# A convolution with three outputs from four products of 171 columns, and work moved into the attention's last unit

## The chip, the cores and the metric

The kernel runs on one core of a Trainium2 chip. The metric is the device time of one execution in microseconds, as the median of several. The core has five engines that run side by side and wait for each other through semaphores: TensorE (PE, matmuls; PEld is its weight load), VectorE (DVE), ScalarE (ACT), GpSimd (POOL) and SyncE (SP), which here issues nearly all DMA transfers. Each engine, SP too, works through its own instructions in order.

## The reference

Inputs are x (4 batches, 1024 tokens, 512 features), a context tensor (4, 2048, 512), a side column (4, 1024, 1) and weights. Three blocks follow each other, and each adds its input and is normalised over the 512 features:

```python
x = _layernorm(x + attn(x))     # 32 heads of 16; q, k and v are two chained linear layers each
x = _layernorm(x + xattn(x, ctx_1024, fside))
x = _layernorm(x + ffn(x))      # quantised activations, ternary weight
```

The middle block treats the 1024 tokens as 512 hidden channels and 512 cell channels, and the 512 features as positions:

```python
xp = concatenate([hid, z1h], axis=2)              # one more position in front
out = uss + conv_general_dilated(xp, weight) + bias   # 512 -> 2048 channels, kernel size 2
it, ot, gt, ft = split(out, 4, axis=1)
ct = sigmoid(ft) * z0c + sigmoid(it) * tanh(gt)
ht = sigmoid(ot) * tanh(ct)
```

So the convolution is, for every output position s, w0 x[s] + w1 x[s+1] over a padded row of 513 positions, where w0 and w1 are 512x2048 matrices.

## The kernel before

**Attention.** `attention` runs 32 units, one for each batch and group of four heads, with a step u = -1 ahead of them. A unit's inner loop has 32 half steps h (line 638). In each, TensorE makes scores twice: once with queries on partitions (`nat`, line 421, for the row maxima of the next unit, reduced on VectorE in line 437) and once with keys on partitions (`scores`, line 491), from which ScalarE makes exponentials (line 502); every fourth h, `weigh` (line 517) multiplies these by the values. Fill pieces go between: projections of queries and keys (line 346), of values (line 371), and in the last units output projections of batches 0 and 2 (`out_piece`, line 400, which calls `Handed.project`, line 180). The last unit, u = 31, has no `nat` work left: it runs the branch of line 610, 16 steps i with two score groups each and a weighing at every even i, and no fill.

**What goes round a unit.** The four stages of `normalise` (line 536) move a unit's denominators out and back through DRAM, multiply on GpSimd (line 564) and store the result to `attn_d` with eight DMAs (line 574). Packed projections lie in tiles of the pool `packs`; DMAs spread them into the query and key tiles (line 332).

**The hand-over.** `Handed` holds what is prepared for the tail during the attention: the convolution's first weight tile (`load_conv(0)`, at i = 1 of the last unit), its tap sums on GpSimd (`sum_taps`, line 147), the small constants and the ternary weight (`load_rest`, line 149). `outs` (line 587) lists the output projections that the attention does: all eight tiles of batch 0 and five of batch 2. After the last weighing, lines 675 to 681 put out, in this order, the first stage of the last unit's `normalise`, the first norm of batch 0 (`first_norm`, line 119: statistics, a square root on ScalarE, eight normalisations on VectorE), and the other stages.

**The tail.** A list of due times (`after(steps, work)` and `step()`) puts side work between the steps of TensorE's work. Lines 902 to 911 begin it: two context loads, output projection of tile 5 of batch 2, the convolution's operands of batch 0 (`fir_parts`), tiles 6 and 7, the load of batch 1's attention, the first norm of batch 2. Then, for the batches (0, 2) and after that for (1, 3): four rounds t; a round is four gates g for each of the two batches, so eight gates of 128 output channels by 512 positions. In each round the next weight tile is loaded at its first gate and its taps are summed two gates later (line 936). After the fourth gate of a batch, `combine` (line 777) makes the cell and hidden channels with six GpSimd operations and a tanh on ScalarE, and then loads the context tile that comes two later (`load_ctx(k + 2)`), for the context tiles have two buffers. After four rounds, `feed_forward` runs for the 16 tiles of both batches; between the two pairs come the output projections of batches 1 and 3.

**A gate.** The convolution gets two outputs from three products of 256 columns. With pairs of neighbouring positions (x0, x1) and the next x2, `fir_parts` makes x0 - x1, x1 and x2 - x1 on VectorE and ScalarE, and `sum_taps` makes w0 + w1. The first output is w0 (x0 - x1) + (w0 + w1) x1, the second w1 (x2 - x1) + (w0 + w1) x1. So a gate (line 756) is three products over four blocks of 128 channels, 12 matmuls of 256 columns. VectorE adds the first two products to the context tile (line 767) and the third, common to both, to both halves (line 768), and ScalarE applies the gate's function (line 769). The two accumulator tags `ps_c` and `ps_a` have two buffers each.

Of the kernel before, what the change touches and what calls it, by code (L numbers as in the profile page):

```python
# [14 lines left out]
P = 128  # L15
# [5 lines left out]
VW = HD + 1  # L21
EPS = 1e-5
# [29 lines left out]
class Handed:  # L52
# [3 lines left out]
    def __init__(self, tc, a, shared, attn_d, eps):  # L56
        self.eps = eps
        self.nc, self.a, self.shared, self.attn_d = tc.nc, a, shared, attn_d
        self.big, self.y, self.stats = {}, {}, {}
# [59 lines left out]
    def first_norm(self, b):  # L119
# [3 lines left out]

        def part(t0):
            if t0 == 0:
                made.extend(self.norm_stats(self.stats[b], self.shared, f"1_{b}"))
# [4 lines left out]
        return x1, [lambda t0=t0: part(t0) for t0 in range(0, NT, 2)]  # L131

    def load_conv(self, m, pool):


        if m % 2 == 0:
            w = self.shared.tile([P, 6, S], F32, tag="qk3", name=f"w{m}")
        else:
            w = pool.tile([P, 6, S], F32, tag="w", name=f"w{m}")
        w = w.rearrange("p a s -> p (a s)").rearrange("p (i k o) -> p i k o", i=FT, k=3)  # L140
# [4 lines left out]
    def sum_taps(self, w):  # L145
        for i in range(FT):
            self.nc.gpsimd.tensor_add(w[:, i, 2, :], w[:, i, 0, :], w[:, i, 1, :])

    def load_rest(self):
# [7 lines left out]
        nc.gpsimd.dma_start(self.w_f, a["ternary_wT"].rearrange("(t p) f -> p t f", p=P))  # L157
# [7 lines left out]
    def prepare_rest(self):  # L165
        nc = self.nc
        nc.gpsimd.tensor_scalar_add(self.w_f, self.w_f, -1.0)
# [28 lines left out]
def attention(ctx, tc, a, attn_d, ident, shared, hand):  # L196
# [35 lines left out]
    for n, pool in ((3, shared), (1, once)):  # L232
        t = pool.tile([P, 2 * n, S], F32, tag=f"qk{n}", name=f"qk{n}")
        for i in range(n):
# [3 lines left out]
            k_ts.append(t[:, n + i, :])  # L238

# [10 lines left out]
    packs = ctx.enter_context(tc.tile_pool(name="packs", bufs=1))  # L250
# [19 lines left out]
    for which, (w, v, dst) in enumerate((("wq", "vq", b_q), ("wk", "vk", b_k), ("wv", "vv", None))):  # L270
# [22 lines left out]
        if which == 2:  # L293
            bias()
            b_d = dpool.tile([D], F32, tag="b_v", bufs=1, name="b_vd")
            nc.gpsimd.dma_start(b_d.rearrange("(t p) -> p t", p=P), dst)
            nc.gpsimd.dma_start(b_v, b_d.partition_broadcast(P))
# [84 lines left out]
    packed_of = {}  # L382

    def qk_pieces(p, which):


        def piece(t0, n):
            if t0 == 0:
                packed_of[p, which] = packs.tile(
                    [P, S], F32, tag=f"packed{which}", name=f"packed{p}_{which}"  # L390
                )
            project(p, which, t0, n, packed_of[p, which])

        parts = [(0, 176), (176, 176), (352, 176), (528, 176), (704, 160), (864, 160)]
        return [lambda part=part: piece(*part) for part in parts]
# [191 lines left out]
    outs = [(0, t) for t in range(NT)] + [(2, t) for t in range(5)]  # L587
# [3 lines left out]
    for piece in qk_pieces(0, 0) + qk_pieces(0, 1) + folds[:5]:  # L591
        piece()

    for u in range(-1, NU):
# [15 lines left out]
        if u == -1 or u + 1 == NU:  # L610
            total, done = len(fill), 0
            for i in range(HS // 2):
# [8 lines left out]
                if u >= 0 and i % 2 == 1:  # L621
                    weighing.append((u, i // 2))
                if i == 1 and u >= 0:
# [364 lines left out]
```

## Time and profile before

| | us |
|---|---|
| median of 3 runs | 2502.4 (2501.43 to 2502.85) |
| the profiled execution | 2499.28 |
| its span, first to last instruction | 2497.5 |

The granted TensorE clock was 0.999 of full speed. Read from the trace by stage, in us from the span's start:

| stage | from | to | PE busy | DVE busy | ACT busy | POOL busy |
|---|---|---|---|---|---|---|
| convolution of batches 0 and 2, most of it | 2040 | 2136 | 96.00 | 35.86 | 22.05 | 40.69 |
| their feed-forward | 2136 | 2202 | 62.51 | 60.98 | 22.33 | 6.72 |
| output projections of 1 and 3 | 2202 | 2257 | 55.00 | 42.92 | 1.80 | 5.39 |
| convolution of batches 1 and 3 | 2257 | 2424 | 167.00 | 65.59 | 36.04 | 62.32 |
| their feed-forward | 2424 | 2497.5 | 62.03 | 65.19 | 22.59 | 6.69 |

An fp32 matmul stands in the trace as two matmul records, each with its weight load. Matmuls are pipelined, so the busy time of one record is longer than the spacing of two; the spacing is read from the chain of work that ended last, whose pieces give a start, a length and how many records it holds. In groups, the numbers after the bar are the busy time in all and the mean in ns of one, and behind the second bar stands the engine's idle time just before them and what ended it.

### The profile page before, as it was taken

The numbers are of one execution on the slowest core, as the hardware profiler recorded it, in microseconds if no ns is written. First come the engines' busy times: TensorE is split into PE (matmuls) and PEld (weight loads), VectorE is DVE, ScalarE is ACT, GpSimd is POOL, SyncE is SP. The second block draws the span as 40 slices with busy tenths as digits, with TensorE's granted clock in tenths as the row PEclk, the third lists the DMA queues.
The fourth block names the chain that finished last, engine by engine and source line by source line (L and its number), as shares of the span: only waits on it lengthen the run. The fifth ranks groups of instructions, "written<-read, shape, count | busy, mean of one in ns | idle before, by whom it ended". The sixth has DMA issues, their size and how long they took to land.

```text
span 2497.5 us, 58830 instructions
## 1 busy us (share of the span) xinstructions
PE 2476.3 (99%) x24956; PEld 1766.8 (71%) x24956; DVE 1670.5 (67%) x2055; ACT 1309.9 (52%) x2560; POOL 293.5 (12%) x230
## 2 busy tenths in 40 slices
PE   9999999999999999999999999999999999999998
PEld 6677777777777777777777776777776688548874
DVE  3767777776777777777777777777775433875348
ACT  1166666666666666666666666666656411401132
POOL 2000000000000000000000002000021245102530
PEclk9999999999999999999999999999999999999999
DMA  7001111111110211111111114011111323230301
GB/s 246 17 11 20 20 25 53 21 24 20 25 24 16 58 21 20 20 22 23 20 23 22 23 22 134 16 25 21 54 45 50 115 85 118 89 147 31 120 19 68
DMA packets 80086, 120.71 MB, mean 48 GB/s; under 512 B 38560, under 2 KB 38560, under 8 KB 79824
## 3 DMA queue, kind: packets, MB, share of 16 engines
q1 hardware_dynamic: 78608, 114.59, 16.2%
q8 instruction: 196, 3.21, 0.5%
q0 software_dynamic: 640, 1.31, 0.2%
q10 hardware_dynamic: 576, 1.05, 0.1%
q14 instruction: 66, 0.54, 0.1%
HBM read 80.77 MB, written 18.35 MB: 40 GB/s over the span
## 4 chain that ended last, share of the span: by engine, by line
PE 94%; DVE 5%; DMA 0%; issue 0%; ACT 0%; SPq 0%; POOL 0%; DVEq 0%; POOLq 0%
PE nat L421 21%; PE av L517 19%; PE st L491 18%; PE proj L346 10%; PE pc L765 9%; PE v L371 5%; PE pa L765 4%; PE po L185 4%; PE fold L307 1%; PE pf L844 1%; DVE y L849 1%; DVE y L875 1%; DVE y L115 1%; DVE stats L850 1%; DVE xq L830 1%; PE fold L361 1%
## 5 line engine op out<-in xcount | busy, mean ns | idle before, releaser
L437 DVE TENSOR_REDUCE mx<-nat 128x2 f32<-128x1024 f32 x1008 | 1187.5, 1219 | 453.8 <-PE st L491 424.2
L502 ACT ACTIVATE at<-st 128x512 f32<-128x512 f32 x2016 | 1042.7, 602 | 609.9 <-PE st L491 605.7
L421 PE MATMUL nat<-qk 32*128 32x512 f32 x4032 | 1012.8, 614 | 1.0 <-DVE mx L437 1.0
L491 PE MATMUL st<-qk 32*128 32x256 f32 x8064 | 998.9, 387 | 0.0
L491 PEld LDWEIGHTS st<-qk 32*128 32x128 f32 x8064 | 656.1, 184 | 46.0 <-issue 3.6
L517 PE MATMUL av<-at,v_sb 128*32 128x256 f32 x8192 | 497.4, 382 | 0.6 <-ACT at L502 0.6
L421 PEld LDWEIGHTS nat<-qk 32*128 32x128 f32 x4032 | 343.3, 184 | 171.4 <-DVE mx L437 117.2
L517 PEld LDWEIGHTS av<-at,v_sb 128*32 128x32 f32 x8192 | 241.4, 109 | 221.6 <-ACT at L502 90.2
L564 POOL TENSOR_TENSOR o_n<-o_sb,rbc 128x512 f32<-128x512 f32 x64 | 94.9, 1506 | 1643.9 <-DMA rbc<-rec_d 1356.6
L346 PE MATMUL proj<-xT,w_qk 128*128 128x176 f32 (+1 forms) x1536 | 270.2, 320 | 0.7 <-ACT w_qk L312 0.7
L346 PEld LDWEIGHTS proj<-xT,w_qk 128*128 128x128 f32 x1536 | 223.7, 189 | 64.6 <-ACT at L502 60.0
L765 PE MATMUL pc<-xf,w 128*128 128x256 f32 x1024 | 231.9, 379 | 2.9 <-DVE u L767 2.9
L765 PEld LDWEIGHTS pc<-xf,w 128*128 128x128 f32 x1024 | 194.3, 190 | 30.4 <-DVE u L767 3.3
L769 ACT ACTIVATE u<-u,b_c 128x512 f32<-128x512 f32 x64 | 46.2, 722 | 207.9 <-DVE u L768 207.9
L767 DVE TENSOR_TENSOR u<-pc,u 128x512 f32<-128x512 f32 x64 | 44.2, 691 | 142.3 <-PE pc L765 134.4
L371 PE MATMUL v<-w_v,xT 128*128 128x256 f32 x512 | 126.0, 391 | 0.0
L765 PE MATMUL pa<-xf,w 128*128 128x256 f32 x512 | 120.9, 379 | 0.0
L844 PE MATMUL pf<-w_f,xq_t 128*128 128x512 f32 x256 | 115.6, 595 | 4.5 <-DVE y L849 3.0
L185 PE MATMUL po<-w_o,big 128*128 128x256 f32 (+1 forms) x360 | 117.5, 477 | 0.0
L371 PEld LDWEIGHTS v<-w_v,xT 128*128 128x128 f32 x512 | 92.5, 189 | 34.4 <-ACT at L502 16.6
L530 DVE TENSOR_TENSOR o_sb<-av,o_sb 128x256 f32<-128x256 f32 x128 | 54.3, 424 | 92.5 <-PE av L517 92.5
L765 PEld LDWEIGHTS pa<-xf,w 128*128 128x128 f32 x512 | 97.3, 190 | 13.2
(94 smaller groups left out, 1111.6 us busy)
## 6 DMA issues: line engine op xcount, KB each, us to landing
qk<-packed SPq DMA_DIRECT2D x256, 64.0 KB
w<-in_conv_wT SPq DMA_DIRECT2D x32, 512.0 KB
u<-in_ctx SPq DMA_DIRECT2D x16, 1024.0 KB
xT<-in_xT SPq DMA_DIRECT2D x16, 512.0 KB
rbc<-rec_d SPq DMA_DIRECT2D x128, 64.0 KB
attn<-o_n SPq DMA_DIRECT2D x256, 32.0 KB
big<-attn SPq DMA_DIRECT2D x4, 2048.0 KB
y<-in_x SPq DMA_DIRECT2D x4, 2048.0 KB
```

The costliest lines, as they stand in the source:

```text
L185: nc.tensor.matmul(pt, attn_t[:, f, t * P : (t + 1) * P], self.w_o[:, f, cols], start=f == 0, stop=f == FT - 1)
L346: nc.tensor.matmul(pt[:, 0:n], w[:, f, gg * P : (gg + 1) * P], xts[b][:, f, cols], start=f == 0, stop=f == FT - 1)
L371: nc.tensor.matmul(pt, xts[b][:, f, t * P : (t + 1) * P], w_v[:, f, cols], start=f == 0, stop=f == FT - 1)
L421: nc.tensor.matmul(pts[n], q_ts[u % 4][r : r + 32, qt * P : (qt + 1) * P], k_ts[u % 4][r : r + 32, kh * 512 : kh * 512 + 512], start=True, ...
L437: nc.vector.tensor_reduce(mxs[u][:, qt, 2 * pair : 2 * pair + 2, kh], pt, AX.X, ALU.max, negate=True)
L491: nc.tensor.matmul(st[:, k * QW : k * QW + QW], k_ts[u % 4][r : r + 32, kt * P : (kt + 1) * P], q_ts[u % 4][r : r + 32, qq * QW : qq * QW ...
L502: nc.scalar.activation(at, st, AF.Exp, scale=0.25)
L517: nc.tensor.matmul(av[32 * j : 32 * j + 32, :], v_sb[b % 2][:, kt, c * VW : c * VW + 32], ats[u, 2 * i + n // 2, j][:, n % 2 * QW : n % 2 ...
L530: nc.vector.tensor_add(o, av, o)
L564: nc.gpsimd.tensor_mul(o_n[:, :, half * 256 : half * 256 + 256], o_sb[:, cols].rearrange("p (s e) -> p e s", e=2), rbc[:, cols].rearrange( ...
L765: nc.tensor.matmul(dst, w[:, i, tap, o : o + P], xf[:, tap, i, :], start=i == 0, stop=i == FT - 1)
L844: nc.tensor.matmul(pt, xq_ts[b, t][:, f, :], hand.w_f[:, f, :], start=f == 0, stop=f == FT - 1)
```

## The change

Three outputs now come from four products of 171 columns (a third of 513, the padded row). For positions x0, x1, x2 of a triple and the next x3 the four products are p0 = w0 (x0 - x2), p1 = w1 (x3 - x1), m = (w0 + w1)(x1 + x2) and n = (w0 - w1)(x2 - x1). The outputs are p0 + m/2 + n/2, m/2 - n/2 and p1 + m/2 + n/2. A gate is 16 matmuls of 171 columns. The context tiles and `load_ctx` go to `Handed` and have 513 columns, with the last set to zero by GpSimd; the weight tiles have four taps; the gate's VectorE work is four operations.

```diff
-        for dst, tap in ((pt[:, 0, :], 0), (pt[:, 1, :], 1), (pa, 2)):
-            if tap == 1 and between:
+        ends = ps_c.tile([P, 2, 256], F32, tag="c", name=f"pc{b}_{t}_{g}")
+        mids = ps_a.tile([P, 2, 256], F32, tag="a", name=f"pa{b}_{t}_{g}")
+        for tap in range(4):
+            if tap == 2 and between:
                 between()
+            pt = (ends, mids)[tap // 2][:, tap % 2, 0:TR]
             for i in range(FT):
-                nc.tensor.matmul(dst, w[:, i, tap, o : o + P], xf[:, tap, i, :], start=i == 0, stop=i == FT - 1)
-        ug = u[:, g, :].rearrange("p (m e) -> p e m", e=2)
-        nc.vector.tensor_add(ug, pt, ug)
-        nc.vector.tensor_add(ug, pa.unsqueeze(1).to_broadcast([P, 2, 256]), ug)
+                nc.tensor.matmul(pt, w[:, i, tap, o : o + P], xf[:, tap, i, :], start=i == 0, stop=i == FT - 1)
+
+        ug = u[:, g, :].rearrange("p (m e) -> p e m", e=3)
+        outer = ug[:, 0:3:2, :]
+        nc.vector.tensor_add(outer, ends[:, :, 0:TR], outer)
+        m, n = (mids[:, i, 0:TR] for i in range(2))
+        both = n.unsqueeze(1).to_broadcast([P, 2, TR])
+        nc.vector.scalar_tensor_tensor(outer, both, 0.5, outer, ALU.mult, ALU.add)
+        nc.vector.scalar_tensor_tensor(ug[:, 1, :], n, -0.5, ug[:, 1, :], ALU.mult, ALU.add)
+        all3 = m.unsqueeze(1).to_broadcast([P, 3, TR])
+        nc.vector.scalar_tensor_tensor(ug, all3, 0.5, ug, ALU.mult, ALU.add)
```

The taps and the operands:

```diff
     def sum_taps(self, w):
-        for i in range(FT):
-            self.nc.gpsimd.tensor_add(w[:, i, 2, :], w[:, i, 0, :], w[:, i, 1, :])
+        for tap, op in ((2, ALU.add), (3, ALU.subtract)):
+            for i in range(FT):
+                self.nc.gpsimd.tensor_tensor(w[:, i, tap, :], w[:, i, 0, :], w[:, i, 1, :], op)
+
+    def fir_parts(self, b, x1, pool):
...
+        xf = pool.tile([P, 4, FT, TR], F32, tag="xf", name=f"xf{b}")
+        x = x1[:, 0:FT, :].rearrange("p t (m e) -> p t e m", e=3)
+        x0, x1, x2 = (x[:, :, e, :] for e in range(3))
+        tt = self.nc.vector.tensor_tensor
+
+        def first():
+            tt(xf[:, 0, :, :], x0, x2, ALU.subtract)
+            tt(xf[:, 2, :, :], x1, x2, ALU.add)
+
+        def second():
+            tt(xf[:, 3, :, :], x2, x1, ALU.subtract)
+            self.nc.vector.memset(xf[:, 1, :, TR - 1 : TR], 0.0)
+            tt(xf[:, 1, :, 0 : TR - 1], x0[:, :, 1:TR], x1[:, :, 0 : TR - 1], ALU.subtract)
```

Work moved into the attention's last units: the output projections of tiles 5 to 7 of batch 2 as six half pieces, the statistics of batch 0's first norm (at h = 5 of unit 30), its normalisation and operands (steps i from 3 on), and the first context load.

```diff
-    outs = [(0, t) for t in range(NT)] + [(2, t) for t in range(5)]
+    outs = [(0, t) for t in range(NT)] + [(2, t) for t in range(NT)]
...
+                if u >= 0 and i % 2 == 0 and out_pieces:
+                    out_pieces.pop(0)()
+                if u >= 0 and i > 2 and firsts:
+                    firsts.pop(0)()
...
+                if i == 3 and u >= 0:
+                    hand.load_ctx(0, None)
...
+                if h == 5 and u == 30:
+                    hand.x1[0], firsts = hand.first_norm(0)
+                    firsts.pop(0)()
+                    hand.xf[0], parts = hand.fir_parts(0, hand.x1[0], shared)
+                    firsts.extend(parts)
...
-    for part in hand.first_norm(0)[1]:
+    hand.x1[2], parts = hand.first_norm(2)
+    for part in parts:
         part()
...
-    x1[0] = hand.big[0].rearrange("p (t s) -> p t s", t=NT)
-    load_ctx(0)
     load_ctx(1)
     big1 = bigs.tile([P, NT * (D + 1)], F32, tag="big", name="big1")
-    project_out(2, (5,))
-    fir_parts(0)
-    project_out(2, (6, 7))
-    hand.load_attention(1, big1)
-    first_norm(2)
+    firs[2], parts = hand.fir_parts(2, x1[2], fir)
+    for m, part in enumerate(parts):
+        after(m + 1, part)
+    after(5, lambda: hand.load_attention(1, big1))
```

The first norm of batch 2 is therefore the one put out after the last weighing. For batches 1 and 3 the operands' two parts come as separate side work, due within five steps (batch 1) or three (batch 3) of the norm's start.

Three more edits concern where things lie and by which queue they come. The packed projections move from their own pool into two more rows of the tile that holds queries and keys of three of four units (`qk3`), and the weight tiles of even number use that tile's place. The value bias goes through DRAM on SP's queue, after the first projections, instead of on GpSimd's. The ternary weight is loaded by SP as integers and turned to fp32 in the GpSimd operation that subtracts one, where a GpSimd DMA converted it before; the scratch for GpSimd's DMAs is set to 2048.

```diff
-        nc.gpsimd.dma_start(self.w_f, a["ternary_wT"].rearrange("(t p) f -> p t f", p=P))
+        nc.sync.dma_start(self.w_f.bitcast(mybir.dt.int32), a["ternary_wT"].rearrange("(t p) f -> p t f", p=P))
...
-        nc.gpsimd.tensor_scalar_add(self.w_f, self.w_f, -1.0)
+        nc.gpsimd.tensor_scalar_add(self.w_f, self.w_f.bitcast(mybir.dt.int32), -1.0)
...
-        t = pool.tile([P, 2 * n, S], F32, tag=f"qk{n}", name=f"qk{n}")
+        t = pool.tile([P, 8 if n == 3 else 2, S], F32, tag=f"qk{n}", name=f"qk{n}")
...
+        if n == 3:
+            packs = t[:, 6:8, :]
...
+    nc.sync.dma_start(b_d.rearrange("(t p) -> p t", p=P), b_vc)
+    nc.sync.dma_start(b_v, b_d.partition_broadcast(P))
```

## The prediction

> **What bounds the kernel now.** I read the page first (busy shares, then the chain that ended last), then the chain in order of time over the convolution and over the start, then the timeline where the attention ends, then busy time by window.
>
> ```profile
> PE 94%; DVE 5%; DMA 0%; issue 0%; ACT 0%; SPq 0%; POOL 0%; DVEq 0%; POOLq 0%
> ...
> L765 PE MATMUL pc<-xf,w 128*128 128x256 f32 x1024 | 231.9, 379 | 2.9 <-DVE u L767 2.9
> ...
> L765 PE MATMUL pa<-xf,w 128*128 128x256 f32 x512 | 120.9, 379 | 0.0
> ```
>
> The chain is TensorE for 94%. In the convolution its only idle time is 2.9 us, once. Every fp32 matmul has two records, so 1,024 + 512 records are 768 matmuls: 64 gates of 12. The busy means (379 ns) overlap; a price has to be read from the chain, which gives the pace:
>
> ```profile
> 33.67 14.16 PE proj L346 x96
> ...
> 2202.14 54.93 PE po L185 x128
> 2257.07 3.45 PE pc L765 x16
> 2260.52 1.73 PE pa L765 x8
> 2262.25 3.45 PE pc L765 x16
> ```
>
> A gate is 3.45 + 1.73 = 5.18 us, 0.216 us a record of 256 columns; 512 columns take 54.93/128 = 0.429. So a column costs (0.4291 - 0.2158)/256 = 0.833 ns and a record 2.5 ns besides. The first row is the nearest to what comes: the 48 projection matmuls of the start, of 176 and 160 columns (on average 170.7), each record with its own 128x128 weight load.
>
> Where the attention ends:
>
> ```profile
> 1955.98 10.57 PE L185 MATMUL po<-w_o,big 128*128 128x512 f32 x24
> ...
> 1973.88 0.94 SPq L754 DMA_DIRECT2D u<-in_ctx  x2
> ...
> 1979.02 0.69 DVE L767 TENSOR_TENSOR u<-pc,u 128x512 f32<-128x512 f32 x1 [7.88 <-DMA u<-in_ctx]
> ...
> 1979.77 3.72 PE L765 MATMUL pc<-xf,w 128*128 128x256 f32 x16 [2.86 <-DVE u L767]
> ```
>
> TensorE does three output projections, starts gate 0 at 1966.4, and after two gates stands still for 2.86 us: both PSUM buffers are full, VectorE waits for the first context tile, and that load stood in SP's queue behind the last unit's attention stores.
>
> **The gates (the large term).** A gate becomes 16 matmuls of 171 columns, 32 records. By the two slopes a record is 2.5 + 171 x 0.833 = 145 ns, so 4.64 us; by the projection row 14.16/96 = 147.5 ns, so 4.72 (that row holds the slow first record). Gain per gate 0.54 or 0.46, times 64: **-34.4** or -29.3 us. I take -34.4, since the row's excess belongs to its first record, and keep both.
>
> [...] 216 ns is the whole spacing today, and projections ran at 147.5 ns a record with a load for each (the page's mean load of line 346, 189 ns, is longer than that spacing, so it overlaps). [...]
>
> VectorE takes the gate out of PSUM with four operations instead of two. From 256 elements at 424 ns (L530) and 512 at 691 (L767): 157 ns + 1.043 an element. So 342, 342, 171 and 513 elements: 0.51 + 0.51 + 0.34 + 0.69 = 2.06 us against 1.38. That lies beside 4.64 us of TensorE, except where nothing follows. After the very last product of a pair of batches three of them (1.54 us) stand ahead of the feed-forward's first quantisation, where one (0.69) stood:
>
> ```profile
> 2136.34 0.70 DVE u L768
> 2137.70 0.81 ACT xq L828
> ```
>
> +0.85 twice, **+1.7 us**. Ends: 0, if VectorE's backlog there is recovered[...].
>
> The scalar_tensor_tensor form and a stride of three elements are not in the trace. A stride of two is: L767 takes 691 ns, as the contiguous L849 does. [...]
>
> **GpSimd.** Eight tap operations per weight tile instead of four (1.27 each): 10.2 us for 5.0. Behind them in its queue stand combine's operations, behind these the next context load:
>
> ```profile
> 2025.93 5.00 POOL L147 TENSOR_TENSOR w<-w 128x512 f32<-128x512 f32 x4 [7.07 <-DMA w<-in_conv_wT]
> ```
>
> Counted from the start of an eight-gate round (about 2011): taps from +15 to +25; combine about 7.5, so the load goes out at +33, lands some 5 us later (the first context loads took that) at +38. VectorE asks for it at 37.1 + 2.3 = +39.4; TensorE stalls only two gates after the round begins, at +46.4. The memset of one column adds 0.1. Cost 0, with 8 us of cover. The first round is tighter: its weight tile is issued behind the attention stores, about 18 us in, taps end near +35, the context goes out near +42 and lands near +47, against +46.4. I take **+1 us**, ends 0 and +4.
>
> **The moved output projection.** Six half pieces go into the last unit. There ScalarE is nearly full, and weighings follow each other every 4.27 us (8.55 for two, in the second view):
>
> ```profile
> 1930.00:1940.00 10.00, 10.00 (x156) 6.93 (x152) 1.11 (x3) 9.54 (x20) 2.64 (x2) 1.00 0.11 30
> ```
>
> (A window: busy PE, weight load, VectorE, ScalarE, GpSimd, clock, DMA share, GB/s.) The chain there:
>
> ```profile
> 1928.44 1.96 PE av L517 x32
> ...
> 1936.99 1.96 PE av L517 x32
> ```
>
> TensorE's own work there is about 3.93 us (av 1.86, two scores' 2.07), so 0.34 is free. A piece in earlier units costs 1.94 with its change of layout; 1.94 - 0.34 = 1.6, six times +9.6. At the boundary 10.4 us (1955.98 to 1966.38) go, and the 2.86 us stall goes, since context 0 is now loaded during the unit: one SP issue of 0.4 us behind the denominator transfers (there until 1928.5), its memset on an idle GpSimd. The doubled taps of the first weight tile run there from 1923.7 to about 1934, ahead of the attention scaling, which waits for its data until 1937.4. Late next is the second context tile: issued some 18 us after the last weighing, landing near +23, with gate 4 asking at 23.2 and a stall only from 27.9. Norm and tap operands of batch 0 (before: 1956.5 to 1965.6) run on a VectorE busy a tenth in that window. Sum 9.6 - 10.4 - 2.9 = **-3.7**, ends -5 (more hidden) and -2.
>
> **The early deviations** cost ScalarE a table load, 0.30 us and a load back (each 1.28 in the trace) amid exponentials in unit 30, and put 0.63 us of bn_aggr ahead of VectorE's reductions. ScalarE has 0.7 to 1.8 us idle in every 3.83; four score buffers cover more. Ends 0 and +2.9, taken **+1**. A gain is excluded: it adds work there, and what it takes away lay under the output projection.
>
> **At no cost.** The value bias goes to SP behind sixteen row transfers (issued until 55.4); its store took 8.4 us and its broadcast 6.4, so it lands near 70; first use 82.0. The next xT, queued behind it, slips from 55.5 to about 64, first read near 166. Ternary weights: one SP issue more in unit 24, where the 5.4 us GpSimd pass had an idle engine. Operands of the other batches: four VectorE operations of 684 elements (0.87) for two of 1.23 and a ScalarE copy, in rounds with slack; their two steps end before the second batch's gates. Attention reload five gates later: first read at 2202. Packed projections now inside the query/key tile: same lifetimes.
>
> **Sum.** -34.4 + 1.7 + 1 - 3.7 + 1 = -34.4 us. The profiled execution took 2499.28 (span 2497.5 and 1.8 around it), so 2464.9; on the median of 2502.4, 3.1 above it, **2468.0**.
>
> **Rivals.**
> 1. GpSimd's chain becomes a wait in every round: contexts 10 us later than reckoned, beyond the 8 us cover, 2 us in six rounds, 2480. For: the taps double while the round shrinks by 4.3 us. Against: the margin. 0.10.
> 2. More is hidden: pieces vanish in ScalarE's waits, deviations and end free: -34.4 - 5 = -39.4, 2463. 0.08.
> 3. Slower: VectorE becomes the bound through 12-byte strides. Its other work in the second convolution is (65.6 - 32 x 1.38)/32 = 0.67 us a gate, so it decides from 3.97 us a gate, 1.9 times my price, and the kernel is slower from about 4.5[...]. For: the stride is unseen. [...] 0.04.
> 4. The change doesn't do what it says: packed rows in one tile with queries and keys bring false waits, 2 us in 32 projections, +64 - 34, 2532. Against: queries and keys of three units share that tile already, and the projections show 0.7 us idle in all. 0.03.
>
> My forecast has 0.73, 0.02 is left for anything else that just cancels. Of no change one can tell 0.2%, 5 us. Faster 0.91, same 0.02, slower 0.07. Range: bounds of the sum, -39.4 and -29.3 + 2.8 + 4 - 2 + 2.9 = -21.6, so 2463 to 2481; a little more below for the profile's offset: 2460 to 2480.
>
> **What would show it.** A gate at 4.64 us in the chain, records 145 ns apart; VectorE's four operations 2.06 us; no TensorE idle before gate 2; last unit near 47 us instead of 37; feed-forward beginning 0.85 later after the last product. Wrong if records stand at 190 ns, if chain rows in the convolution name GpSimd or the context load, or if VectorE's strided operations exceed 1 us.

## The result and the profile after

| | before | after |
|---|---|---|
| median of 4 runs, us | 2502.62 (2501.43 to 2502.89) | 2486.51 (2485.63 to 2487.75) |
| profiled execution, us | 2499.28 | 2487.75 |
| its span, us | 2497.5 | 2486.0 |
| mean granted TensorE clock | 0.999 | 0.996 |

The ratio is 0.9937, with an interval of 0.992 to 0.9954: the kernel is 16.1 us faster where 34.4 were predicted, and 2486.5 lies outside the predicted 2460 to 2480. The two profiled executions are only 11.5 us apart, because that of before lay 3.3 us under its median and that of after 1.2 us above; the ledger below adds up to 11.5.

From the page of the changed kernel: the shares of the chain that ended last, and the two groups of the gates (columns as before: line, engine, operation, tiles, shapes, count | busy us, mean ns | idle us before and its releaser):

```profile
PE 91%; DVE 5%; POOL 2%; DMA 0%; ACT 0%; issue 0%; SPq 0%; DVEq 0%; POOLq 0%
...
L792 PE MATMUL pc<-xf,w 128*128 128x171 f32 x1024 | 161.9, 310 | 6.0 <-DVE u L796 4.4
L792 PE MATMUL pa<-xf,w 128*128 128x171 f32 x1024 | 161.4, 310 | 0.0
```

GpSimd, at 0% of the chain before, now has 2% of it, and the matmuls of the convolution waited 6.0 us, where they waited 2.9. The chain in order of time shows a gate's two halves and, between them, where the chain leaves TensorE (start, us, what):

```profile
1981.85 2.33 PE pa L792 x16
1984.18 2.35 PE pc L792 x16
...
1986.58 1.50 POOL o_n L592
...
1992.24 5.98 DMA w<-in_conv_wT
...
1998.43 9.92 POOL w L161 x8
2008.35 1.05 POOL u L814
...
2014.28 1.27 POOL y L822
...
2016.83 4.24 PE pc L792 x16
```

A half gate is 2.333 us, a record 145.8 ns, a gate 4.667: the large term of the prediction came as reckoned. But from 1986 to 2017 the end is set by a weight tile's load, the eight tap operations on it, and `combine` behind them in GpSimd's queue. The first half gate after that takes 4.24 us instead of 2.33.

To see where the gain went, I cut both traces at the first TensorE record of each stage (a feed-forward's is its first product, `pf`, so the first transposes count to the convolution; the difference is taken before rounding):

| stage | before | after | difference |
|---|---|---|---|
| start, and units 0 to 23 | 1515.2 | 1514.6 | -0.6 |
| unit 24 | 58.71 | 63.13 | +4.4 |
| units 25 to 29 | 293.31 | 293.63 | +0.3 |
| unit 30 | 56.68 | 60.80 | +4.1 |
| last unit, first to last weighing record | 31.82 | 41.45 | +9.6 |
| from there to gate 0 | 10.71 | 0.98 | -9.7 |
| convolution 1 (32 gates) | 169.76 | 161.82 | -7.9 |
| feed-forward 1 | 65.83 | 67.08 | +1.3 |
| projections | 54.93 | 54.93 | 0 |
| convolution 2 (32 gates) | 166.64 | 152.90 | -13.7 |
| feed-forward 2 and end | 73.97 | 74.65 | +0.7 |

64 gates should have given 64 x (5.18 - 4.667) = 32.8 us, 16.4 for each convolution, and the first should have gained 2.9 more from its old stall. It gained 7.9. Two more places lost time that the prediction had at nothing: unit 24, and unit 30 beyond its one piece of 1.9 us. The next views show the stalls.

**Unit 24.** The timeline (start, duration in us, engine, line, operation, tiles, shapes, count [idle before it and its releaser]), GpSimd first, then VectorE, then TensorE:

```profile
1546.56 5.38 POOL L204 TENSOR_SCALAR w_f<-w_f 128x2048 f32<-128x2048 int32 x1
...
1545.26 1.35 DVE L210 TENSOR_TENSOR sc<-sc 128x1 f32<-128x1 f32 x1
...
1546.91 3.31 DVE L213 TENSOR_TENSOR sc<-sc 128x1 f32<-128x1 f32 x1
...
1550.21 3.66 DVE L465 TENSOR_REDUCE mx<-nat 128x2 f32<-128x1024 f32 x3
...
1551.47 0.70 PE L449 MATMUL nat<-qk 32*128 32x512 f32 x2 [3.35 <-DVE mx L465]
```

and before, the same pass and the operation that is L213 above:

```profile
1549.66 5.37 POOL L167 TENSOR_SCALAR w_f<-w_f 128x2048 f32<-128x2048 f32 x1 [2.45 <-DMA w_f<-in_ternary_wT]
...
1547.80 0.16 DVE L176 TENSOR_TENSOR sc<-sc 128x1 f32<-128x1 f32 x1
```

L213 took 3.31 us beside GpSimd's pass over the ternary weights, where it took 0.16 before, and with L210 it held up VectorE's maxima. Before, that pass began 3.1 us later, since it waited for a GpSimd DMA, and these operations had gone by.

**Gate 8.** VectorE's timeline:

```profile
2013.00 0.69 DVE L826 BATCH_NORM_STATS2 stats<-y 128x6 f32<-128x512 f32 x1 [6.12 <-POOL y L820]
2015.58 0.69 DVE L827 BATCH_NORM_STATS2 stats<-y 128x6 f32<-128x512 f32 x1 [1.88 <-POOL y L822]
2016.18 0.59 DVE L796 TENSOR_TENSOR u<-pc,u 128x342 f32<-128x342 f32 x1
```

The two statistics of `combine`'s result stand in VectorE's queue ahead of the next gate's first operation. They waited 6.12 and 1.88 us for GpSimd, and the gate's products stayed in PSUM so long that TensorE stood still for 2.50 us. At the end of this convolution the same two statistics wait again, for 0.92 and 1.88 us, behind the taps of the fifth weight tile, and 2.64 us of TensorE follow at the first transposes:

```profile
2126.78 0.69 DVE L827 BATCH_NORM_STATS2 stats<-y 128x6 f32<-128x512 f32 x1 [1.88 <-POOL y L822]
```

Two stalls are of other kinds. Ahead of gate 3 a convolution operand of batch 2 (line 176) waited 5.98 us for GpSimd's `o_n` (1.89 us of TensorE). At gate 36 (0.97 us) VectorE had the four convolution operands of batch 3 in one row ahead of the gate's sums, 5 us in all: three took 1.1 us each and the last 1.95, beside the first operation of `combine` on GpSimd.

**The clock.** Busy time by window (start:end, TensorE, weight load, VectorE, ScalarE, GpSimd, then granted clock, DMA share, GB/s), right after the stall at gate 8 and after one at the third tile's turn in feed-forward 1, with an undisturbed window last:

```profile
2017.00:2021.00 4.00, 4.00 (x17) 4.00 (x18) 3.83 (x7) 0.72 (x1) 1.09 (x1) 0.60 0.97 345
2143.00:2147.00 4.00, 4.00 (x6) 1.56 (x6) 3.86 (x4) 1.30 (x2) 2.99 (x4) 0.57 0.00 0
2150.00:2160.00 10.00, 10.00 (x33) 4.95 (x32) 9.51 (x28) 4.28 (x7) 0.00 (x0) 1.00 0.54 218
```

After these stalls TensorE ran at half clock for 3.41 us: the granted clock is 0.50 from 2016.82 to 2020.23 and from 2143.11 to 2146.52, so 0.60 and 0.57 over the 4 us of the windows, and 1.00 in the undisturbed one. The half gate behind the first transposes took 4.01 us (at 2132.56) where it takes 2.33, 1.7 us more. There were four such stretches: in unit 24, at gate 8, behind the first transposes and in feed-forward 1. The last cost nothing that can be seen: the stage took 67.08 us with it, and 67.08 to 67.16 in experiments 1, 4 and 6, whose profiles have none there. TensorE does not set the pace of that stage.

### The profile page after: what moved, and what is told of

It is laid out like the page before. It is cut to its first block, busy times and chain, and to the rows that moved or that the text cites. A ratio compares the mean times of both kernels' runs of the same rounds, so it can differ in the third digit from the quotient of the medians.

```text
span 2486.0 us, 60152 instructions
## 1 busy us (share of the span) xinstructions
PE 2452.5 (99%) x25492; PEld 1781.1 (72%) x25492; DVE 1748.6 (70%) x2198; ACT 1306.5 (53%) x2558; POOL 333.5 (13%) x275
## 4 chain that ended last, share of the span: by engine, by line
PE 91%; DVE 5%; POOL 2%; DMA 0%; ACT 0%; issue 0%; SPq 0%; DVEq 0%; POOLq 0%
PE nat L449 22%; PE av L545 19%; PE st L519 18%; PE proj L383 10%; PE v L408 5%; PE po L222 5%; PE pa L792 5%; PE pc L792 5%; PE fold L344 1%; PE pf L878 1%; POOL w L161 1%; DVE y L116 1%; DVE y L883 1%; DVE y L909 1%; DVE xq L864 1%; DVE stats L884 1%
## 5 line engine op out<-in xcount | busy, mean ns | idle before, releaser
L530 ACT ACTIVATE at<-st 128x512 f32<-128x512 f32 x2016 | 1042.4, 603 | 625.5 <-PE st L519 610.0
L792 PE MATMUL pc<-xf,w 128*128 128x171 f32 x1024 | 161.9, 310 | 6.0 <-DVE u L796 4.4
L792 PE MATMUL pa<-xf,w 128*128 128x171 f32 x1024 | 161.4, 310 | 0.0
L792 PEld LDWEIGHTS pc<-xf,w 128*128 128x128 f32 x1024 | 153.6, 191 | 7.7 <-DVE u L796 4.9
L792 PEld LDWEIGHTS pa<-xf,w 128*128 128x128 f32 x1024 | 153.7, 191 | 0.0
L408 PEld LDWEIGHTS v<-w_v,xT 128*128 128x128 f32 x512 | 92.5, 189 | 34.4 <-ACT at L530 16.6
L222 PEld LDWEIGHTS po<-w_o,big 128*128 128x128 f32 x384 | 70.3, 190 | 49.2 <-issue 31.6
```

The costliest lines, as they stand in the source:

```text
L222: nc.tensor.matmul(pt, attn_t[:, f, t * P : (t + 1) * P], self.w_o[:, f, cols], start=f == 0, stop=f == FT - 1)
L408: nc.tensor.matmul(pt, xts[b][:, f, t * P : (t + 1) * P], w_v[:, f, cols], start=f == 0, stop=f == FT - 1)
L530: nc.scalar.activation(at, st, AF.Exp, scale=0.25)
L792: nc.tensor.matmul(pt, w[:, i, tap, o : o + P], xf[:, tap, i, :], start=i == 0, stop=i == FT - 1)
```

## The experiments

Theory after this reading: the gates gain what was predicted, and the rest is order. GpSimd's doubled and moved work is waited for through VectorE's queue, the moved pieces hide nothing, and half clock followed the stalls of 2.37, 2.50, 2.64 and 3.35 us. Rivals: the price of VectorE's three-element stride; the GpSimd pass itself; the place of tiles in SBUF. Medians are of 4 or 5 runs; before took 2501.0 to 2502.3 beside them.

**1. The ternary pass later (`wf_late`).**

```diff
     def prepare_rest(self):
-        nc.gpsimd.tensor_scalar_add(self.w_f, self.w_f.bitcast(mybir.dt.int32), -1.0)
...
+                if h == 24 and u == 24:
+                    hand.prepare_w_f()
```

> The changed kernel with one edit: the GpSimd pass that turns the ternary weight to fp32 and subtracts one is put out three half steps later in unit 24, behind VectorE's tiny operations on the scale instead of ahead of them. Theory [...]: those operations with two SBUF inputs stood behind the 5.4 us GpSimd pass, which now starts earlier because its data come sooner. Then the 3.35 us idle of TensorE in unit 24 shrinks to 0.5 or less and the kernel is 3 to 4.5 us below the changed kernel (2486.5): 2482 to 2483.5. Rival (late data): VectorE waited for the scale's own load, now behind 1 MB on SP's queue; then the wait stays and the time is 2486.

Measured 2486.74, no gain; unit 24 took 62.8. The pass did not move:

```profile
1542.63 2.97 POOL L594 TENSOR_TENSOR o_n<-o_sb,rbc 128x512 f32<-128x512 f32 x2
1545.56 5.38 POOL L217 TENSOR_SCALAR w_f<-w_f 128x2048 f32<-128x2048 int32 x1
```

It begins as `o_n` ends, as in the changed kernel (1546.56), though it was put out three half steps later: nothing else stands in GpSimd's queue. The experiment told nothing of the theory, but something of queues: the later place in the program delayed nothing here, since the work in front of it on the same engine ended no later.

**2. VectorE's scale operations later (`sc_later`).** So the other partner had to move: VectorE was busy for 18.66 of the 24 us from 1538 to 1562 in the changed kernel, and with so much in its queue I expected a later place to be a later time.

```diff
     def prepare_rest(self):
         nc = self.nc
         nc.gpsimd.tensor_scalar_add(self.w_f, self.w_f.bitcast(mybir.dt.int32), -1.0)
+    def prepare_scale(self):
+        nc = self.nc
...
                 if h == 21 and u == 24:
                     hand.prepare_rest()
+                if h == 4 and u == 25:
+                    hand.prepare_scale()
```

> The seven one-column operations that VectorE makes of the quantising scale go from unit 24's half step 21 to unit 25's half step 4; GpSimd's pass over the ternary weights stays. Theory: two of the seven, of two operands in SBUF each, stood 1.35 and 3.31 us behind GpSimd's passes and held up VectorE's maxima, so TensorE; away from the passes they take 0.15 us, the 3.35 us stall goes and the stretch at half clock behind it too: unit 24 from 63.1 to about 58.7, 2482. Rival: the GpSimd pass itself delays something in unit 24 (it starts 3.1 us earlier than before): unit 24 stays at 63, 2486.5.

Measured 2482.08 (2480.78 to 2482.70), the theory's value. Unit 24 took 57.84, 0.9 us less than before even, where the first of these operations had stood 2.20 us beside `o_n`.

```profile
1545.61 5.36 POOL L204 TENSOR_SCALAR w_f<-w_f 128x2048 f32<-128x2048 int32 x1
...
1572.37 0.16 DVE L214 TENSOR_TENSOR sc<-sc 128x1 f32<-128x1 f32 x1
```

The pass is where it was, and the same operation (here line 214, begun at 1572.37 instead of 1546.91) takes 0.16 us. So this operation with two SBUF operands took 3.31 us beside the pass and 0.16 away from it. By what way the pass held it up is not shown; L213 ended 1.7 us ahead of the pass's recorded end. A one-operand operation beside GpSimd's work (line 211 in the changed kernel) took 0.14, as it does away from it (here line 212).

**3. The move undone (`undo`).** Four products stay; `outs` ends at five tiles of batch 2 again, and the boundary is as before:

```diff
-    outs = [(0, t) for t in range(NT)] + [(2, t) for t in range(NT)]
+    outs = [(0, t) for t in range(NT)] + [(2, t) for t in range(5)]
...
-    hand.x1[2], parts = hand.first_norm(2)
+    hand.x1[0], parts = hand.first_norm(0)
...
+    load_ctx(0)
     load_ctx(1)
     big1 = bigs.tile([P, NT * (D + 1)], F32, tag="big", name="big1")
-    firs[2], parts = hand.fir_parts(2, x1[2], fir)
-    for m, part in enumerate(parts):
-        after(m + 1, part)
-    after(5, lambda: hand.load_attention(1, big1))
+    project_out(2, (5,))
+    firs[0], parts = hand.fir_parts(0, x1[0], hand.shared)
+    for part in parts:
+        part()
+    project_out(2, (6, 7))
+    hand.load_attention(1, big1)
+    first_norm(2)
```

> The four products stay; the last projection, the first norm and the first context go back behind the attention, where they stood before. The prediction's step for the move (-3.7 us) says that this kernel is 3.7 us slower than the changed one: about 2490. Theory from the ledger of the changed kernel: the move gained 9.7 us between the last attention product and gate 0 and the 2.9 us stall of the early gates, and cost 9.6 us of pieces in the last unit, 1.9 us of a piece and 2.2 us of deviations in the unit before it, and 1.9 us of a new stall ahead of gate 3; that is +3.0 us, so undoing it gives 2482 to 2486, no slower than the changed kernel, with the last unit near 31.8 us again and some 10.7 us between the last attention product and gate 0.

Measured 2479.03 (2478.49 to 2479.14): 7.5 us faster than the changed kernel, more than the theory said and on the other side of the prediction. Unit 30 fell by 4.1, the last unit by 9.6, the boundary rose by 9.7, as in the ledger; but convolution 1 fell by 5.1, to 156.76. No stall at gate 3, and at gate 8 only this:

```profile
2009.41 2.60 PE L781 MATMUL pc<-xf,w 128*128 128x171 f32 x16 [1.31 <-DVE u L785]
```

The half gate behind it takes 2.60 us (2.50 is usual in this view) and not some 4.2: no half clock here. One thing is not as before in this kernel: the first context tile now lies in the shared pool, and its load, which waits for nothing, went out at 29.8 us. So the old stall of 2.86 us is absent without the move too: the prediction's gain of 2.9 for it needed only the tile's place.

Why the pieces hide nothing is in the chain in order of time, changed kernel:

```profile
1938.42 2.21 PE av L545 x32
1940.62 1.92 PE po L222 x8
...
1944.62 2.21 PE av L545 x32
```

Weighings with a piece are 6.20 us apart. Before, two took 8.55, so 4.275 each: a piece costs 1.93 us, its full length. The chain in the last unit before is TensorE alone; there was no idle 0.34 us in a step, although the busy times that I added (1.86 + 2.07) leave that much.

**4. Deviations later (`dev_late`).** The statistics of batch 0's first norm move from unit 30 to the first step of the last unit (shortened: the whole block under the condition moves).

```diff
-                if h == 5 and u == 30:
+                if i == 0 and u >= 0:
                     hand.x1[0], firsts = hand.first_norm(0)
                     firsts.pop(0)()
```

> The changed kernel with one edit: the deviations of batch 0's first norm are put out at i = 0 of the last unit instead of h = 5 of unit 30. Theory (table load among exponentials): unit 30 falls from 60.8 back to 56.6 us, and the last unit, where ScalarE has some 2 us free in every 6.2, grows by 0 to 2.9: 1.2 to 4.1 us below the changed kernel, 2482.4 to 2485.3. Rival (unit 30 was held up by VectorE's statistics or by anything else than the square root): the loss moves along or stays, 2486.

Measured 2486.30, no gain. Unit 30's stall (2.12 us, "po <- ACT at L530") went, and one of 1.24 us came in the last unit. Over both units 0.6 us is gained where 1.2 to 4.1 was expected: the table load and its return (1.28 us each, at 1926.78 and 1929.84) meet exponentials there too.

**5. Taps two gates later (`taps_late`).**

```diff
-                        after(3, lambda w=w_next: hand.sum_taps(w))
+                        after(5, lambda w=w_next: hand.sum_taps(w))
```

> The changed kernel with one edit: a weight tile's taps are made two gates later, behind the first batch's combine in GpSimd's queue instead of ahead of it. Theory (GpSimd's doubled taps hold combine back, and VectorE stands at combine's statistics, with the gates' sums behind them): the 2.50 us idle of TensorE ahead of gate 8 and the 2.64 ahead of the first transposes go, and with them the slow clock that followed each (some 1.7 us a time): 5 to 9 us below the changed kernel, 2477.5 to 2481.5. Rival (VectorE's own longer work in the gate, with its 12-byte strides, is what is late): both stalls stay, 2486. Third case (taps themselves become late for the next round's third product): new TensorE waits at gates 8, 16, 24, slower than 2486.

Measured 2483.68 (2481.93 to 2489.02), 2.8 us where 5 to 9 was expected. With `combine` put out ahead of the taps the stall at gate 8 is gone, convolution 1 falls to 158.53, and gate 36's falls under 0.4. The one at the first transposes stays (2.43): now the taps of the fifth weight tile run from 2115.9 to 2126.5, beside the second norm, and VectorE's normalising there takes 1.02 us an operation instead of 0.50.

**6. Another order of the tail's pools (`pools`).** The pools for contexts and weights come first, so that batch 2's operands lie in other bytes than the attention's buffers.

```diff
+    wp = ctx.enter_context(tc.tile_pool(name="convw", bufs=1))
     fir = ctx.enter_context(tc.tile_pool(name="fir", bufs=1))
     bigs = ctx.enter_context(tc.tile_pool(name="bigs", bufs=1))
-    wp = ctx.enter_context(tc.tile_pool(name="convw", bufs=1))
```

> The changed kernel with one edit: the tail's SBUF pools in another order, so that batch 2's operands lie over the exponentials' tiles, which are free after the last weighing, and not over the pool that holds the denominators' broadcast, which GpSimd reads until 13 us later. Theory (false wait through reused SBUF): VectorE's 5.98 us wait for GpSimd and TensorE's 1.89 us ahead of gate 3 go. But the stall ahead of gate 8 hangs on GpSimd's chain, which is timed by the weight tile's arrival and not by TensorE, so it grows by as much: 2485.5 to 2486.5, no gain alone. Rival (gate 8's stall is timed by the gates before it): 2 us below the changed kernel, 2484.5.

Measured 2489.84, slower than the changed kernel. Gate 3's stall went, so the place of the tile had made that wait. But gate 8's became 7.06 us: `o_n` took 3.91 us beside VectorE's operands instead of 2.94, the weight load behind its stores went out 2.3 us later, and the taps ended at 2011.5 instead of 2008.3. It is GpSimd's chain that times gate 8.

**7. The stride (`dense`).** A gate's context slices become runs of neighbours:

```diff
-        ug = u[:, g, :].rearrange("p (m e) -> p e m", e=3)
+        ug = u[:, g, :].rearrange("p (e m) -> p e m", e=3)
```

> Leaves the computation changed in one part: a gate's three context slices are three runs of 171 neighbouring elements and not every third element each, so values meet the wrong context. Measures the price of the 12-byte stride on VectorE: theory, the four operations of a gate fall from 0.63, 0.63, 0.39, 0.87 us to the row's 0.51, 0.51, 0.34, 0.69; the sigmoid on ScalarE stays. Of the time it moves only the stalls that a gate's tail makes (gate 8's is GpSimd's): 0 to 2 us. If instead VectorE's pace sets the gates' 4.67 us, conv1 and conv2 fall by more than 5 us: 2480 or less.

VectorE's groups by form from 1990 to 2125 us (of 29 gates each), changed kernel:

```profile
L802 DVE SCALAR_TENSOR_TENSOR u<-pa,u 128x513 f32<-128x513 f32 x29 | 25.3, 873 | 1.0
...
L800 DVE SCALAR_TENSOR_TENSOR u<-pa,u 128x171 f32<-128x171 f32 x29 | 11.3, 389 | 0.0
```

and with neighbours:

```profile
L802 DVE SCALAR_TENSOR_TENSOR u<-pa,u 128x513 f32<-128x513 f32 x29 | 20.1, 693 | 1.0
...
L800 DVE SCALAR_TENSOR_TENSOR u<-pa,u 128x171 f32<-128x171 f32 x29 | 9.5, 327 | 0.0
```

From 171 and 513 elements: (873 - 389)/342 = 1.42 ns an element with the stride of 12 bytes, (693 - 327)/342 = 1.07 without, and 2.05 us a gate without it, the row's price of the prediction. The four operations take 2.52 us a gate with it, where the prediction's row had 2.06. The time, 2485.70 (2482.09 to 2487.48), hardly moved: the stride costs VectorE 0.47 us a gate, beside 4.67 of TensorE.

**8. Products m and n first (`mids_first`).** Then one operation of 0.63 us follows the last product of a gate. (Not shown: the two halves of the operands change places as well.)

```diff
-        for tap in range(4):
-            if tap == 2 and between:
+        for tap in (2, 3, 0, 1):
+            if tap == 0 and between:
                 between()
...
-        nc.vector.tensor_add(outer, ends[:, :, 0:TR], outer)
         m, n = (mids[:, i, 0:TR] for i in range(2))
...
         nc.vector.scalar_tensor_tensor(ug, all3, 0.5, ug, ALU.mult, ALU.add)
+        nc.vector.tensor_add(outer, ends[:, :, 0:TR], outer)
```

> Products m and n are made first, s and d last, and so behind the last product of a gate stands one VectorE operation of 0.63 us and not three of 0.63, 0.39 and 0.87. Theory: the feed-forward's first stalls (2.37 us and 2.32 us) are the gate's tail on VectorE; with 1.26 us less in it they fall to about 1.1 us each, and where a stall of over 2.3 us drew a stretch at half clock behind it, 1.7 us goes with it: 2480 to 2484. Rival: the turns wait for the quantising chain and not for the gate's tail: the stalls stay, 2486. Rival 2: the order of products moves nothing but makes m and n wait for a convolution window that comes last: slower by up to 2.

Measured 2482.37 (2481.84 to 2484.40), the expected gain for another reason. The stalls at the third tile's turn stay (2.31 and 2.31): VectorE is behind by then, and the last gate's sigmoid, which waits for it, stands in ScalarE's queue ahead of the quantising (it begins at 2137.64, the quantising at 2138.27). What went is 2.3 us in convolution 1 and 2.4 in convolution 2. The stalls at gates 8 and 36 are gone and the one at the first transposes fell to 1.13, by what way is not shown; gate 3's grew to 3.40.

**9 to 12. Together.** First (`undo_qt`), the undone move with taps later (the fifth weight tile's put out only in the projection stage) and the third tile quantised ahead of the last gate's tail:

```diff
-                        after(3, lambda w=w_next: hand.sum_taps(w))
+                        after(27 if (n, t) == (0, 3) else 5, lambda w=w_next: hand.sum_taps(w))
...
+            if ahead and t == 2:
+                after(1, lambda: quantise(b, 2))
...
-        quantise(*tiles[2])
```

> The kernel with the move undone (2479.0), and two edits of order: the doubled taps come two gates later (for the first weight tile of the second convolution, only in the projection stage), and the third tile's quantising is put ahead of the last gate's tail instead of behind it. Theory: what is left of stalls is GpSimd's and VectorE's order: 1.3 us at gate 8, 1.0 at gate 36, 2.24 at the first transposes (half of it stays), and 2.36 and 2.30 at the third tile's turn, the first of these with a stretch at half clock of 1.7 us behind it; together some 9: 2469 to 2472. Rival: VectorE is booked out at the end of a pair of batches whatever the order, so the stalls only move: 2476 or more.

Measured 2479.69: no gain. Convolution 1 fell by 3.1, but feed-forward 1 rose from 66.7 to 72.6. With the scale operations and the order of products besides (`best_undo`):

> As the kernel with the move undone and the two edits of order, and besides it the scale's one-column operations in unit 25 (-4.4 as measured alone) and products m and n first (-4.1 as measured alone, of which some 1 to 2 is left where the other edits have taken the stalls): 2463 to 2467. Rival: the gains are of the same stalls and do not add: 2470 or more.

Measured 2471.71 (2470.74 to 2473.90), with the same 72.6 in feed-forward 1. And with the move kept, the same edits and batch 2's operands put out together after gate 2 (`best_move`):

> The changed kernel with its move kept, and with all edits of order (taps two gates later, third tile's quantising early, scale operations in unit 25, m and n first, batch 2's convolution operands put out together after gate 2). Theory: what the move costs by itself is the ledger's 4.1 us in unit 30 and 9.6 in the last unit less 9.7 at the boundary, 4.0 us; the other 3.5 to 5 us that undoing it gained were stalls at gates 3 and 8, which the edits take away too. So 4 us above the version without the move: 2467 to 2471. Rival: the move's loss in the first convolution can't be ordered away: 7 us or more above it.

Measured 2475.63 (2475.37 to 2477.69), 3.9 us above the version without the move, where 4.0 was expected: that is what the move costs by itself. The other 3.6 us that undoing it had gained were stalls, and order removes them. In the version without the move, in feed-forward 1:

```profile
2127.01 11.19 POOL L161 TENSOR_TENSOR w<-w 128x512 f32<-128x512 f32 x8
...
2127.06 1.50 DVE L116 TENSOR_SCALAR y<-y,mv,rstd 128x512 f32<-128x512 f32 x1
2128.48 1.48 DVE L857 TENSOR_SCALAR xq<-xq 128x512 f32<-128x512 f32 x1
```

The taps meant for the projection stage run here: the mistake of the first experiment again. Beside them VectorE's normalising takes 1.50 us, alone 0.50, and the two quantising operations 1.48 and 1.37 instead of 0.42 and 0.48. The last version holds them back by their own load and leaves the early quantising out (`best4`):

```diff
+    def fifth():
+        nonlocal w_next
+        w_next = hand.load_conv(4, wp)
+        hand.sum_taps(w_next)
...
-                        w_next = hand.load_conv(4 * n + t + 1, wp)
-                        after(3, lambda w=w_next: hand.sum_taps(w))
+                        if (n, t) == (0, 3):
+                            after(26, fifth)
+                        else:
+                            w_next = hand.load_conv(4 * n + t + 1, wp)
+                            after(5, lambda w=w_next: hand.sum_taps(w))
```

> The kernel with the move undone, scale operations in unit 25, m and n first, taps two gates later, and no early quantising. The fifth weight tile's load (and so its taps) goes out in the second convolution's projection stage, where before only the taps were put out late. Theory: putting out the taps late did not delay them, since GpSimd has nothing else queued: they ran in the feed-forward (2133 to 2144) and stretched VectorE's operations beside them (normalising 1.36 us instead of 0.50), which cost the 5.8 us that the first feed-forward stage grew by; held back by their own load they leave it at 66 to 67 us: 2465 to 2467. Rival: it was the early quantising or the order of products that cost the feed-forward its 5.8 us in the last version: then this one, without the first and with the second, tells which: at 72 us again it is the order of products, and 2471.

Measured **2465.79** (2464.55 to 2466.02), ratio 0.9853 (0.9836 to 0.9869): 36.5 us under before and 20.7 under the changed kernel. The taps wait for their data, and VectorE's normalising in the feed-forward has its length (two operations in 0.99 us):

```profile
2191.68 11.21 POOL L161 TENSOR_TENSOR w<-w 128x512 f32<-128x512 f32 x8 [66.78 <-DMA w<-in_conv_wT]
...
2126.72 0.99 DVE L116 TENSOR_SCALAR y<-y,mv,rstd 128x512 f32<-128x512 f32 x2
```

Feed-forward 1 is at 66.79, the convolutions at 151.46 and 151.11, the granted clock at 0.999. This version differs from the one before it in the early quantising too, so that edit's share of the 5.8 us is not separated by this run alone. In the second feed-forward, where no taps run, early quantising took 0.9 us off and put 0.7 on the convolution ahead of it.

## Why the prediction was wrong

| step | predicted | measured |
|---|---|---|
| gates | -34.4 | 64 x (5.18 - 4.667) = -32.8 |
| VectorE's tail ahead of the feed-forward | +1.7 | 1.25 + 0.68 = +1.9 |
| GpSimd's chain | +1 | stalls at gate 8 and the first transposes, 5.1, and two half-clock stretches, 3.4: +8.5 |
| moved projection and boundary | -3.7 | 1.92 + 9.63 - 9.73 - 2.86 = -1.0, and the stall at gate 3, 1.9: +0.9 |
| early deviations | +1 | +2.2 |
| ternary weights | 0 | unit 24, +4.4 |
| operands of the other batches | 0 | stall at gate 36, +1.0 |

The right column adds up to -13.9; the spans differ by 11.5, and 2.4 us stay unassigned, mostly in convolution 2.

**The gates: right.** Records stand 145.8 ns apart, each with a weight load of 128x128. The 2,048 loads take 191 ns each in the trace, longer than that spacing, so they overlap the matmuls, as the projection row had shown. Rival 3, VectorE's stride as the bound, is refuted by 2.52 us a gate and by the stride's removal.

**GpSimd's chain: the step that failed most, +1 predicted and +8.5 measured.** "Cost 0, with 8 us of cover" followed GpSimd's queue only to the next context load. The times in that queue came as reckoned: in the first round the taps ended 33.8 us after gate 0 began (+35 predicted) and the next context load went out at +41 (+42). The context was never late. What was late is `combine`'s result, for which VectorE waits with two statistics ahead of the next gate's operations. I had named what is queued behind the taps on GpSimd, and not what is queued behind the wait on VectorE. Taps put out behind `combine` (experiment 5) took the stall at gate 8 away; undoing the move alone left 1.31 us of it. Rival 1 had the right engine, but at other places than it said, and by another way.

**The ternary weights: wrong by their partner.** "The 5.4 us GpSimd pass had an idle engine" is true of GpSimd. Moving the pass 3.1 us ahead put it beside VectorE's two-operand operations, of which one then took 3.31 us. Moving those operations gave 4.4 us back.

**The move: too hopeful by 0.34 us a piece and by a stall.** Free time on TensorE was got as a difference of busy times; the chain there is TensorE alone. The stall of 2.86 us goes without the move, and the move brings one of 1.9 at gate 3. Its operand waited only because of where its tile lies: experiment 6 laid it elsewhere, and the wait of 5.98 us went. With all stalls ordered away the move still costs 3.9 us, where a gain of 3.7 was predicted.

**The small terms.** The deviations were inside their ends (0 to 2.9). The upper end of 2.8 us for the tail on VectorE, which is in the sum of the range, was my estimate and is shown by no trace. The tail was right in size, but hardly by its mechanism: experiment 8 took 1.26 us off it, and the feed-forwards stayed at 66.78 and 74.66 us (67.08 and 74.65 in the changed kernel). "Rounds with slack" was wrong for the operands of batch 3 at gate 36: the operations priced at 0.87 us took 1.1 and one 1.95. Rival 4, false waits from the packed rows, shows nowhere: start and units 0 to 23 are 0.6 us shorter.

**The sum could be had.** With order mended, and without the move, the kernel gains 36.5 us by the median. That this is near the predicted 34.4 is chance: the prediction's sum had the move in it as a gain.

## What to carry to other kernels

When work on one engine grows, follow each wait for it to the queue of the engine that waits, and ask what stands behind that wait there: cover counted only up to the next transfer was no cover here (stalls of 2.50 us at gate 8 and 2.64 at the first transposes). Work on an idle engine started here when its data was there and the work ahead of it had ended, and not where the program put it (the ternary pass at 1545.56, the taps at 2127.01), so to keep it away from a neighbour hold back its data (the taps at 2191.68), or move the neighbour. Free time in a stage that the chain gave wholly to one engine was none: a piece cost its full 1.93 us, whatever busy times add up to.

## What the hardware showed that I had not expected

**Half clock after short stalls.** In the profiles of before, the changed kernel and the twelve experiments, TensorE stood still for 2.4 us or more 23 times (the first 100 us left out), and 21 of these stalls were followed by a stretch at half clock. Of 34 stalls of 2.0 to 2.4 us, 14 were. The length of the stall does not decide alone: 2.86 us in the profile of before drew nothing, and of 2.37 and 2.32 us in the changed kernel only the first did.

The clock records show how long the half clock lasts and when it begins. These 35 stretches, at a granted clock of 0.50, last 3.41 us or, in six cases, 6.83, and those of one execution begin on one grid: in the changed kernel at 1552.61, 2016.82, 2132.87 and 2143.11 us, which are 136, 34 and 3 times 3.413 us apart. I cut each execution at its own grid into pieces of 3.413 us (the profiles of before and of the last version at the half clock of their last microseconds, for they have no other) and added up TensorE's idle time in each piece that was at full clock. All 33 pieces with 2.0 us or more of it were followed by half clock; of the pieces with 1.76 us or less, some 9600, none was; from 1.79 to 1.91 us it went both ways (2 of 7). So in these traces it matters how a stall falls on the grid: the 2.86 us were split into 1.23 and 1.63, the 2.32 us into 1.16 and 1.16, and the 2.37 us lay in one piece.

Where TensorE sets the pace, a stretch of 3.41 us at half clock costs 1.7 us (a half gate took 4.01 us for 2.33); in the feed-forward it cost nothing (67.08 us with it and without). By that, 2.5 + 1.7, I estimate a stall of 2.5 us to be worth up to about 4 to whoever removes it. In experiment 5 one run took 2481.93 us at a mean granted clock of 0.998 and one 2489.02 at 0.995; whether the place of the grid makes that difference isn't shown, for no run set it.

**VectorE beside GpSimd's taps.** Operations of 512 elements with one large SBUF operand took about three times their length there (1.50 for 0.50 us, 1.48 for 0.42, 1.37 for 0.48); the prediction had not weighed VectorE and GpSimd against each other at all. The quantising operations beside `combine` take 1.31 and 1.37 us as well, even in the last version (at 2120.89 and 2122.24 us), just ahead of a stall of 2.32 us at the third tile's turn. Whether that stall goes when they are parted was not tried.
